# Features of the first layer computed one chunk behind its layernorm, the adjacency diagonal read by one transfer, and the hyperedge table loaded ahead of the feature stores

## The chip, the cores and the metric

One Trainium2 chip, one core. The metric is the device time of one execution in microseconds (us): the median of the runs. Engines are named as in the profile: PE (TensorE, with PEld for its weight loads), DVE (VectorE), ACT (ScalarE), POOL (GpSimd), SP (SyncE, which issues most of the DMAs).

## The reference, cut to what matters

Four graph layers run one after the other on `x` of shape 8 x 2048 x 64, each as `x = x + layer(relu(layernorm(x)))`. Only the start of layer 0 is concerned here.

```python
h = jnp.maximum(_layernorm(x, axis=-1), 0.0)
# layer 0, with H: 2048 nodes x 64 hyperedges
h = x @ W
s = leaky_relu(h @ a_node, 0.2)
logits = where(H.T > 0, s, NEG)          # per batch: 64 hyperedges x 2048 nodes
alpha = softmax(logits, axis=-1)
agg = einsum('ben,bnf->bef', alpha, h)
...
# layer 3 sets adj's diagonal to 1; its degrees and layer 0's deg come from adj
```

## The kernel before, in words

The eight batches are held as four pairs (`NP` = 4, index `q`), each pair with its two 64-wide feature vectors stacked on 128 partitions; the 2048 nodes are cut into four chunks of 512 (`NC`, `CW`, index `ch`) or sixteen tiles of 128 (`NT`, index `t`). A tile framework puts the instructions of each engine in an order of its own, so that work that stands later in the program may be issued between earlier work; each engine then runs its list in order. Blocks under an `If` are not mixed with what stands outside them.

**First stage (`start`, up to 109.6 us).** It has three parts, in this order in the text:

- `layernorm_relu(0, write)`: for each chunk, `norm_parts` centers the four pairs on PE (`center`, tile `bank`), squares and relus them on ACT and DVE (L264, L267, L269), sums the squares on PE (`to_rows`), takes the root on ACT (L272) and the reciprocal on DVE (L273). After its `yield` it spreads that by PE (`from_rows`) and `write` (L553) multiplies on DVE into `hn`. `bank` has six buffers; `xr`, `sq` and `std` have one each.
- `features`: for each chunk, `ph` = `W` applied by feature (four matmuls of 512 columns, copied into `h_t`), then `pn` = the same by node (sixteen of 128 columns, four to a bank, copied into `h_n`). `self.copy` alternates ACT (L172) and DVE (L174).
- `check_adj` and `count_nodes`: the sixteen row blocks of `adj` (1 MB each, four row buffers in `rows`) are loaded by SP (L351). Per block, DVE multiplies the diagonal block by the identity and sums it (`junk`, L352, into `own`), ACT squares the block and sums it (L357), and DVE compares block and square (L358). `squares` has two buffers. Then DVE counts degrees (L362 to L407), PE sums the counts, and a `flag` (L566) is set.

Each `junk`, ACT sum and comparison is followed by a short instruction that reads the accumulator. A register load of `flag` (L2277) then decides the branch. In this execution it is the one with `layer0_pairs`.

**Second stage (`layer0_pairs`).** `aggregate` first stores all of `h_n` to DRAM (`h_rows`, L790, sixteen stores of 256 KB), then forms node scores (L799 to L803) into `score` and `raw`, loads the hyperedge table `HT` into both halves of `cap` (L807, two loads of 512 KB), turns it into caps (L808, L809) and, for each of the four pairs, makes logits by a minimum with `cap` (L818), their maximum (L820), the exponential (L822), transposes and sums. Beside it `ranks`, `hyperedge_keys` (which loads `H`, L520) and `by_rank` make an order of the nodes. `h_rows` is first read by the indirect gathers of POOL (L1797) in the stage after this.

Of the kernel before, what the change touches and what calls it, by code (L numbers as in the profile page):

```python
# [7 lines left out]
F = mybir.dt.float32  # L8
# [5 lines left out]
OP = mybir.AluOpType  # L14
AX = mybir.AxisListType
PSUM = bass.MemoryType.PSUM
# [3 lines left out]
P = 128  # L20
NB = 8
N = 2048
D = 64
NP = NB // 2
NT = N // P
R = P // NP
CW = 512
NC = N // CW
# [99 lines left out]
class Kernel:  # L128
# [36 lines left out]
    def mm(self, out, lhsT, rhs, start=True, stop=True):  # L165
        self.nc.tensor.matmul(out, lhsT, rhs, start=start, stop=stop)  # L166

    def copy(self, out, in_):

        self.flip ^= 1  # L170
        if self.flip:
            self.nc.scalar.copy(out, in_)  # L172
        else:
            self.nc.vector.tensor_copy(out, in_)  # L174
# [164 lines left out]
    def check_adj(self, pool, slots):  # L339


        nc = self.nc
        rows = [slots.tile([P, 2, N], F, name=f"rows{i}", tag=f"q{6 + i}") for i in range(2)]
        squares = slots.tile([P, 2, N], F, name="squares", tag="q8")
        same = pool.tile([P, NT], F, name="same")
        deg = pool.tile([P, NT], F, name="deg")
        own = pool.tile([P, NT], F, name="own")
        junk = pool.tile([P, P], F, name="junk")
        for t in range(NT):
            row, sq = rows[t // 2 % 2][:, t % 2], squares[:, t % 2]  # L350
            nc.sync.dma_start(row, self.a["adj"][t * P : (t + 1) * P])  # L351
            nc.vector.scalar_tensor_tensor(  # L352
                junk, row[:, t * P : (t + 1) * P], 1.0, self.ident, op0=OP.mult, op1=OP.mult,
                accum_out=own[:, t : t + 1],
            )

            nc.scalar.activation(sq, row, AF.Square, accum_out=deg[:, t : t + 1])  # L357
            nc.vector.scalar_tensor_tensor(  # L358
                sq, row, 1.0, sq, op0=OP.mult, op1=OP.is_equal, accum_out=same[:, t : t + 1]
            )  # L360
        bad = pool.tile([P, 1], F, name="bad")
        nc.vector.tensor_reduce(bad, same, axis=AX.X, op=OP.add)  # L362
        nc.vector.tensor_scalar(bad, bad, float(N * NT), None, op0=OP.is_lt)
        nc.vector.tensor_sub(own, deg, own)
        return bad, deg, own
# [178 lines left out]
    def start(self, pool, slots):  # L544

        nc, tc, a = self.nc, self.tc, self.a
        self.deg = pool.tile([P, 2, NT], F, name="deg")
        with tc.tile_pool(reuse_waits="tile", name="k00", bufs=1) as k:
            ww = self.block_diag(k, a["W"], "ww")
            hn = Halves(slots, "hn", ("q0", "q1"), False)  # L550

            def write(q, ch, xr, scale):
                nc.vector.tensor_mul(hn(q)[:, ch * CW : (ch + 1) * CW], xr, scale)  # L553

            self.layernorm_relu(0, write)
            self.features(slots, ww, hn)
            bad, deg, adj_deg = self.check_adj(k, slots)
            flag = pool.tile([1, 1], I32, name="flag")
            with tc.tile_pool(reuse_waits="tile", name="check_ps", bufs=1, space=PSUM) as ps:
                for crowded in self.count_nodes(k, slots, adj_deg):  # L560
                    nc.vector.tensor_max(bad, bad, crowded)
                pt = ps.tile([1, P], F, name="pt")
                nc.tensor.transpose(pt, bad, self.ident)
                one = k.tile([1, 1], F, name="one")
                nc.vector.tensor_reduce(one, pt, axis=AX.X, op=OP.max)
                nc.vector.tensor_scalar(flag, one, 0.0, None, op0=OP.is_gt)  # L566
                nc.vector.tensor_scalar_max(deg, deg, 1.0)
                nc.vector.reciprocal(deg, deg)
                pr = ps.tile([NT, P], F, name="pr")
                nc.tensor.transpose(pr, deg, self.ident)  # L570
                rows = k.tile([NT, P], F, name="rows")
                nc.vector.tensor_copy(rows, pr)
                nc.sync.dma_start(self.rdeg, rows)
        return flag

    def features(self, slots, ww, hn):

        tc = self.tc
        h_t = Halves(slots, "h_t", ("q2", "q3"), False)
        h_n = Halves(slots, "h_n", ("q4", "q5"), True)  # L580
        with (
            tc.tile_pool(reuse_waits="tile", name="h_ps", bufs=3, space=PSUM) as ps,
        ):
            for ch in range(NC):
                for q in range(NP):
                    s = slice(ch * CW, (ch + 1) * CW)
                    ph = ps.tile([P, CW], F, name="ph")
                    self.mm(ph, ww, hn(q)[:, s])
                    self.copy(h_t(q)[:, s], ph)
                for t in range(ch * TC, (ch + 1) * TC):  # L590
                    pn = ps.tile([P, NP, P], F, name="pn")
                    for q in range(NP):
                        self.mm(pn[:, q], hn(q)[:, t * P : (t + 1) * P], ww)
                    self.copy(h_n(t), pn.rearrange("n q f -> n (q f)"))
        self.h = hn, h_t, h_n

    def x_ind(self, slots, k):
# [177 lines left out]
    def aggregate(self, slots, raw, h_t, h_n, fcw, av, both, agg_hi, agg_lo):  # L775
        nc, tc, a = self.nc, self.tc, self.a
        with (
# [7 lines left out]
            for s in range(2):  # L785
                h = slice(s * D, (s + 1) * D)
                nc.vector.tensor_copy(node[h, s : s + 1], self.col("a_node")[h])
                nc.vector.tensor_copy(node[h, 2 + s : 3 + s], self.col("a_gn")[h])
            for t in range(NT):
                nc.sync.dma_start(self.h_rows[t * P : (t + 1) * P, : NB * D], h_n(t))  # L790
            hb = w.tile([P, NT, NB], F, name="hb", bufs=1)

            caps = slots.tile([P, 2, N], F, name="cap", tag="q8")
            cap, score = caps[:, 0], caps[:, 1]
            for ch in range(NC):
                s = slice(ch * CW, (ch + 1) * CW)
                pl = ps.tile([P, CW], F, name="pl")
                self.to_pair_rows(pl, node, lambda q: h_t(q)[:, s])
                nc.scalar.activation(score[:, s], pl, AF.Relu, scale=0.8)  # L799
                nc.vector.scalar_tensor_tensor(  # L800
                    score[:, s], pl, 0.2, score[:, s], op0=OP.mult, op1=OP.add
                )
                nc.scalar.copy(raw[:, s], pl)  # L803

            logits = slots.tile([P, 2, N], F, name="logits", tag="q6")
            for s in range(2):
                nc.sync.dma_start(cap[s * D : (s + 1) * D], a["HT"])  # L807
            nc.vector.tensor_scalar(cap, cap, 0.0, None, op0=OP.is_gt)  # L808
            nc.vector.tensor_scalar(cap, cap, 3e38, NEG, op0=OP.mult, op1=OP.add)  # L809
            aggs = w.tile([P, NP, 2, D], F, name="aggs", bufs=1)  # L810
            nc.gpsimd.memset(aggs, 0.0)
            for q in range(NP):
                lg = logits[:, q % 2]
                for ch in range(NC):
                    s = slice(ch * CW, (ch + 1) * CW)
# [9 lines left out]
                for g in range(NT // 4):  # L825
                    pt = ps1.tile([P, 4, P], F, name="pt")
                    for i in range(4):
                        t = 4 * g + i
# [9 lines left out]
                for s in range(2):  # L838
                    h = slice(s * D, (s + 1) * D)
# [7 lines left out]
                for s in range(2):  # L847
                    h = slice(s * D, (s + 1) * D)
# [20 lines left out]
                for s in range(2):  # L869
                    h = slice(s * D, (s + 1) * D)  # L870
# [7 lines left out]
                for i in range(4):  # L878
                    t = 4 * g + i
# [1057 lines left out]
class Scores:  # L1937
# [27 lines left out]
    def bank(self):  # L1965
        return self.ps.tile([P, CW], F, name="bank", tag="p2")
# [397 lines left out]
```

## Time and profile before

| what | value |
|---|---|
| median of 3 runs | 2153.69 us (2149.0 to 2154.99) |
| profiled execution, its own time | 2148.51 us |
| its span in the trace | 2146.8 us |
| DVE busy, 0 to 81.2 us | 68.9 us |
| ACT busy, 0 to 81.2 us | 50.1 us |
| PE busy, 81.2 to 104.1 us | 22.9 us |
| `flag` set (end of L566) | 109.6 us |
| mean granted TensorE clock | 0.932 |

Times within the execution are microseconds from the first instruction. A row of groups ends in busy time and mean duration of one instruction, then in idle time before them and what ended it. A row of the order in time gives the start, the duration, the engine, the line, the operation and the tiles; in square brackets is the idle time before. A matmul of float32 operands shows in the trace as two PE instructions (the group of `ph` has 32 for sixteen matmuls).

### The profile page before, as it was taken

The numbers are of one execution on the slowest core, as the hardware profiler recorded it, in microseconds if no ns is written. First come the engines' busy times: TensorE is split into PE (matmuls) and PEld (weight loads), VectorE is DVE, ScalarE is ACT, GpSimd is POOL, SyncE is SP. The second block draws the span as 40 slices with busy tenths as digits, with TensorE's granted clock in tenths as the row PEclk, the third lists the DMA queues.
The fourth block names the chain that finished last, engine by engine and source line by source line (L and its number), as shares of the span: only waits on it lengthen the run. The fifth ranks groups of instructions, "written<-read, shape, count | busy, mean of one in ns | idle before, by whom it ended". The sixth has DMA issues, their size and how long they took to land. (4 is left out here: it accounts for less than half of the span.)

```text
span 2146.8 us, 21291 instructions
## 1 busy us (share of the span) xinstructions
PE 1914.5 (89%) x7461; PEld 1153.1 (54%) x7466; DVE 1134.1 (53%) x1932; ACT 714.7 (33%) x1351; POOL 702.4 (33%) x595
## 2 busy tenths in 40 slices
PE   5868999977779999999999998999999999679875
PEld 1425766642237774353443543677777666345432
DVE  7877677737660224424334255698603222249774
ACT  6412555535543440020100201335335333258400
POOL 0000466765300006617357065001000000177770
PEclk8868999988869999999999999999999999879997
DMA  8230333441034360140320401456533443475665
GB/s 320 82 110 4 102 104 118 133 171 43 36 94 134 119 177 14 32 125 0 102 56 5 118 1 60 138 186 235 166 118 125 151 145 131 158 210 162 180 181 180
DMA packets 108797, 253.66 MB, mean 118 GB/s; under 512 B 20912, under 2 KB 21056, under 8 KB 101376
## 3 DMA queue, kind: packets, MB, share of 16 engines
q1 hardware_dynamic: 89264, 181.45, 26.7%
q0 software_dynamic: 17104, 66.47, 10.0%
q10 hardware_dynamic: 2304, 4.20, 0.5%
q8 instruction: 63, 1.03, 0.2%
q14 instruction: 62, 0.51, 0.1%
HBM read 218.30 MB, written 33.78 MB: 117 GB/s over the span
## 5 line engine op out<-in xcount | busy, mean ns | idle before, releaser
L325 ACT CAST adj<-adj_t 128x512 fp32r<-128x512 f32 x384 | 237.3, 619 | 685.9 <-PE pp L166 349.5
L1421 POOL TENSOR_TENSOR acc<-acc,y 128x512 f32<-128x512 f32 x224 | 277.1, 1268 | 444.9 <-DVE y L1416 444.9
L166 PE MATMUL pp<-adj,hi 128*128 128x512 f32 x1280 | 364.4, 404 | 4.4 <-ACT adj L325 4.2
L166 PE MATMUL pk<-q,w 128*128 128x512 f32 (+1 forms) x1024 | 356.5, 609 | 1.8 <-ACT q L1389 1.6
L166 PE MATMUL pp<-adj,lo 128*128 128x512 f32 x1280 | 356.3, 398 | 0.0
L166 PEld LDWEIGHTS pp<-adj,hi 128*128 128x128 f32 x1280 | 241.2, 190 | 77.0 <-issue 16.2
L166 PEld LDWEIGHTS pp<-adj,lo 128*128 128x128 f32 x1280 | 242.7, 190 | 55.6
L166 PEld LDWEIGHTS pk<-q,w 128*128 128x128 f32 (+1 forms) x1024 | 136.2, 188 | 210.2 <-issue 165.9
L1416 DVE SCALAR_TENSOR_TENSOR y<-pk,bias,q 128x512 f32<-128x512 f32 x224 | 157.7, 745 | 142.7 <-PE pk L166 133.2
L166 PE MATMUL acc<-q,ident 128*128 128x512 f32 x416 | 203.4, 615 | 28.4 <-DVE q L2151 16.4
L2061 POOL DMA_INDIRECT ring<-f_rows,near x121 | 140.3, 1160 | 67.5 <-issue 30.2
L166 PEld LDWEIGHTS acc<-q,ident 128*128 128x128 f32 x416 | 76.7, 195 | 104.7 <-issue 47.7
L2165 POOL IOTA q<- 128x2048 int32 x1 | 1.8, 1834 | 316.6 <-PE p L166 316.6
L166 PE MATMUL pp<-adj,x_ind_hi 128*128 128x512 f32 x256 | 94.7, 487 | 2.1 <-DVE q L751 1.9
L166 PE MATMUL bank<-std,from_rows 32*128 32x512 f32 x128 | 45.5, 858 | 54.4 <-DVE std L273 34.5
L1853 POOL TENSOR_TENSOR q<-q,beta 128x512 f32<-128x512 f32 x57 | 67.9, 1192 | 54.6 <-DVE beta L1829 30.8
L1416 DVE SCALAR_TENSOR_TENSOR acc<-pk,bias,q 128x512 f32<-128x512 f32 x32 | 22.6, 746 | 118.1 <-PE pk L166 118.1
L2132 DVE TENSOR_TENSOR q<-ring,e 128x1024 f32<-128x1024 f32 x58 | 70.0, 1218 | 9.3 <-PE acc L166 9.1
L273 DVE RECIPROCAL std<-std 128x512 f32<-128x512 f32 x16 | 53.6, 3351 | 36.7 <-ACT std L272 36.6
L166 PE MATMUL pp<-adj,x_ind_lo 128*128 128x512 f32 x256 | 71.7, 399 | 0.0
L1543 POOL DMA_INDIRECT q<-in_adj_dram,order x15 | 17.2, 1146 | 160.3 <-DVE top L1557 134.0
L166 PEld LDWEIGHTS pp<-adj,x_ind_hi 128*128 128x128 f32 x256 | 48.5, 190 | 38.7 <-issue 23.7
(410 smaller groups left out, 2695.8 us busy)
## 6 DMA issues: line engine op xcount, KB each, us to landing
adj_t<-in_adjT_dram SPq DMA_DIRECT2D x128, 512.0 KB, 3.9
adj_t<-in_adjT_dram SPq DMA_DIRECT2D x128, 256.0 KB, 3.3
rows<-in_adj_dram SPq DMA_DIRECT2D x16, 1024.0 KB, 6.0
q<-x SPq DMA_DIRECT2D x10, 1024.0 KB, 4.8
x<-q SPq DMA_DIRECT2D x9, 1024.0 KB, 4.0
q<-in_embT_dram SPq DMA_DIRECT2D x8, 1024.0 KB, 12.1
x_ch<-in_xT_dram SPq DMA_DIRECT2D x4, 1024.0 KB, 6.0
h_rows<-q SPq DMA_DIRECT2D x16, 256.0 KB, 3.6
```

The source lines that it names most:

```text
L166: self.nc.tensor.matmul(out, lhsT, rhs, start=start, stop=stop)
L273: nc.vector.reciprocal(std, std)
L325: nc.scalar.copy(moving, at[:, i])
L1416: nc.vector.scalar_tensor_tensor(y, pks[b, half], bias[:, b : b + 1], emb[:, b], op0=OP.add, op1=OP.mult,)
L1421: nc.gpsimd.tensor_add(acc, acc, y)
L1543: nc.gpsimd.indirect_dma_start(row, None, self.a["adj"], bass.IndirectOffsetOnAxis(ap=order[:, 1, t : t + 1], axis=0),)
L1853: self.nc.gpsimd.tensor_tensor(x, x, by.unsqueeze(2).to_broadcast([P, NB, D]), op=OP.mult)
L2061: self.nc.gpsimd.indirect_dma_start(to, None, self.kern.f_rows[:], bass.IndirectOffsetOnAxis(ap=index, axis=0))
L2132: nc.vector.tensor_tensor(y.rearrange("n i (b f) -> n i b f", b=NB), block[:, i : i + 2, : NB * D].rearrange("n i (b f) -> n i b f", b=NB) ...
L2165: nc.gpsimd.iota(whole, pattern=[[1, N]], base=0, channel_multiplier=0)
```

## The change

`features` now contains the layernorm's loop. For a chunk it loads `x`, runs `norm_parts` up to its `yield`, computes `ph` of the chunk before, runs the rest of `norm_parts`, and computes `pn` of the chunk before; the last chunk's `ph` and `pn` come after the loop. `bank` has four buffers instead of six, and `ph` and `pn` share four instead of having three each. The copies of chunks 0 to 2 all go to ACT; those of chunk 3 alternate as before. The diagonal of `adj` comes into `own` by one transfer issued by POOL, 128 x 16 single elements, in place of sixteen `junk` instructions. In `aggregate` the two loads of `HT` are issued where the stores of `h_n` were, and the stores come at the beginning of pair 1.

```diff
@@ check_adj
-        junk = pool.tile([P, P], F, name="junk")
+        adj = self.a["adj"]
+        nc.gpsimd.dma_start(
+            own, bass.AP(tensor=adj.tensor, offset=adj.offset, ap=[[N + 1, P], [P * (N + 1), NT]])
+        )
         for t in range(NT):
...
-            nc.vector.scalar_tensor_tensor(
-                junk, row[:, t * P : (t + 1) * P], 1.0, self.ident, op0=OP.mult, op1=OP.mult,
-                accum_out=own[:, t : t + 1],
-            )
@@ start
-            self.layernorm_relu(0, write)
-            self.features(slots, ww, hn)
+            self.features(slots, ww, hn, write)
@@ features
-            tc.tile_pool(reuse_waits="tile", name="h_ps", bufs=3, space=PSUM) as ps,
+            tc.tile_pool(reuse_waits="tile", name="ln", bufs=2) as w,
+            tc.tile_pool(reuse_waits="tile", name="ln_ps", bufs=1, space=PSUM) as ps,
...
+            def copy(ch, to, src):
+
+                if ch < NC - 1:
+                    self.nc.scalar.copy(to, src)
+                else:
+                    self.copy(to, src)
+
+            for ch in range(NC):
+                x = self.load_x(w, 0, ch)
+                xr = w.tile([P, NP, CW], F, name="xr", bufs=1)
+                sq = w.tile([P, NP, CW], F, name="sq", bufs=1)
+                std = w.tile([P, CW], F, name="std", bufs=1)
+                norm = self.norm_parts(ch, x, xr, sq, std, bank, write)
+                next(norm)
+                if ch > 0:
+                    by_feature(ch - 1)
+                next(norm, None)
+                if ch > 0:
+                    by_node(ch - 1)
+            by_feature(NC - 1)
+            by_node(NC - 1)
@@ aggregate
-            for t in range(NT):
-                nc.sync.dma_start(self.h_rows[t * P : (t + 1) * P, : NB * D], h_n(t))
...
+            for s in range(2):
+                nc.sync.dma_start(cap[s * D : (s + 1) * D], a["HT"])
             for ch in range(NC):
...
-            for s in range(2):
-                nc.sync.dma_start(cap[s * D : (s + 1) * D], a["HT"])
...
             for q in range(NP):
+                if q == 1:
+                    for t in range(NT):
+                        nc.sync.dma_start(self.h_rows[t * P : (t + 1) * P, : NB * D], h_n(t))
```

More of the change, by code (lines that the diff above doesn't have):

```diff
@@ L574, in start, with features @@
         return flag
-    def features(self, slots, ww, hn):
+    def features(self, slots, ww, hn, write):
         tc = self.tc
@@ L581, in features, with bank, by_feature, by_node @@
         with (
-            tc.tile_pool(reuse_waits="tile", name="h_ps", bufs=3, space=PSUM) as ps,
-        ):
-            for ch in range(NC):
+            tc.tile_pool(reuse_waits="tile", name="ln", bufs=2) as w,
+            tc.tile_pool(reuse_waits="tile", name="ln_ps", bufs=1, space=PSUM) as ps,
+        ):
+            def bank():
+                return ps.tile([P, CW], F, name="bank", bufs=4)
+            def by_feature(ch):
+                s = slice(ch * CW, (ch + 1) * CW)
                 for q in range(NP):
-                    s = slice(ch * CW, (ch + 1) * CW)
-                    ph = ps.tile([P, CW], F, name="ph")
+                    ph = ps.tile([P, CW], F, name="ph", tag="h", bufs=4)
                     self.mm(ph, ww, hn(q)[:, s])
-                    self.copy(h_t(q)[:, s], ph)
+                    copy(ch, h_t(q)[:, s], ph)
+            def by_node(ch):
                 for t in range(ch * TC, (ch + 1) * TC):
-                    pn = ps.tile([P, NP, P], F, name="pn")
+                    pn = ps.tile([P, NP, P], F, name="pn", tag="h", bufs=4)
                     for q in range(NP):
                         self.mm(pn[:, q], hn(q)[:, t * P : (t + 1) * P], ww)
-                    self.copy(h_n(t), pn.rearrange("n q f -> n (q f)"))
+                    copy(ch, h_n(t), pn.rearrange("n q f -> n (q f)"))
+            def copy(ch, to, src):
[17 more added lines that the diff above has]
+            by_node(NC - 1)
         self.h = hn, h_t, h_n
```

## The prediction

> **What bounds the kernel now.** I read first the busy time of the engines by stretch (columns: length, then busy microseconds and instruction count of PE, PEld, DVE, ACT, POOL, then the granted TensorE clock, the DMA share, GB/s), with stretches cut at events taken from the order in time: a chunk's spread of the reciprocals (21.4, 37.9, 54.4, 68.8), the end of the check of `adj` (81.2), the end of the features (104.1), the flag (109.7), and the wait for `HT`.
>
> ```profile
> core 0: us, PE busy (x) PEld busy (x) DVE busy (x) ACT busy (x) POOL busy (x), PEclk, DMA share, GB/s
> ...
> 21.40:37.90 16.50, 10.01 (x27) 2.79 (x27) 16.50 (x24) 12.84 (x17) 0.00 (x0) 0.81 0.98 374
> 37.90:54.40 16.50, 9.92 (x28) 2.87 (x28) 16.50 (x26) 11.50 (x15) 0.00 (x0) 0.81 0.75 267
> 54.40:68.80 14.40, 10.17 (x24) 2.88 (x24) 14.34 (x22) 9.50 (x13) 0.00 (x0) 0.84 0.83 279
> 68.80:81.20 12.40, 9.74 (x31) 4.26 (x32) 12.40 (x20) 5.58 (x7) 0.00 (x0) 0.72 0.01 2
> 81.20:104.10 22.90, 22.90 (x139) 17.17 (x139) 14.35 (x58) 7.67 (x14) 0.00 (x0) 1.00 0.00 1
> 104.10:109.70 5.60, 1.12 (x7) 0.33 (x5) 4.67 (x45) 0.00 (x0) 0.00 (x0) 0.74 0.01 1
> ...
> 124.00:130.40 6.40, 0.58 (x1) 0.00 (x0) 0.06 (x1) 0.00 (x0) 0.00 (x0) 0.50 0.99 210
> ```
>
> Up to 81.2 us DVE never rests: it bounds. PE works 10 of 16 us there, at a clock of 0.81. From 81.2 to 104.1 PE alone bounds, with the features and nothing else. From 124.0 to 130.4 all five engines stand still while DMA runs at 0.99. The whole program's chain of waits covers only its last instructions, so the chain here is read from the order in time:
>
> ```profile
> 68.84 1.74 PE L166 MATMUL bank<-std,from_rows 32*128 32x512 f32 x8 [4.17 <-DVE std L273]
> ...
> 78.90 2.29 DVE L358 SCALAR_TENSOR_TENSOR squares<-rows,squares 128x2048 f32<-128x2048 f32 x1
> ...
> 83.16 3.60 PE L166 MATMUL ph<-q,ww 128*128 128x512 f32 x8
> ...
> 100.60 3.73 PE L166 MATMUL pn<-ww,q 128*128 128x128 f32 x32
> ...
> 104.18 0.26 PE L166 MATMUL pn<-least,ones 128*128 128x224 bf16 x1
> ...
> 109.47 0.14 DVE L566 TENSOR_SCALAR flag<-one 1x1 int32<-1x1 f32 x1
> ```
>
> A chunk of features is 3.6 + 3.7 us of PE, 7.0 from one `ph` block (83.05) to the next (90.05). DVE's own part of the counting is done at 90.4 (end of L568, from 90.19), but the count's matmul stands behind the features in PE's list and waits until 104.2. In the second stage, from the waits, the order in time and the DMA issues (last column: issue to landing):
>
> ```profile
> DVE cap L808 <- DMA cap<-in_HT_dram: 6.7, 1, 6.7
> ...
> 111.65 9.14 SPq L790 DMA_DIRECT2D h_rows<-q  x16
> 120.83 1.23 SPq L807 DMA_DIRECT2D cap<-in_HT_dram  x2
> ...
> cap<-in_HT_dram SPq DMA_DIRECT2D x2, 512.0 KB, 7.5
> ...
> h_rows<-hb SPq DMA_DIRECT2D x1, 64.0 KB, 3.0
> ```
>
> `HT` is issued after sixteen stores and lands behind their 4 MB; the first maximum (L820) can only follow it.
>
> **What the Trainium skill says.** "ScalarE: Activation LUTs", section "What ACT_TABLE_LOAD costs": 186 ns + 0.833 ns per element for an ACTIVATE with immediates, so 612 ns at 512; the trace's copies take 585, so it agrees. A switch of tables would be dear, but copies at 75.3 us already follow the root of L272 with no load before them, so the moved copies bring none. "TensorE: Matmul & The Clock Gate", section "The HAM clock gate", gives half rate after idling; here PE instructions of 512 columns step by 0.86 us (9.72 to 10.57) in the layernorm and 0.43 in dense features. "DMA: Bandwidth & Descriptors", section "Rules for kernel authors": a strided last dimension is one descriptor per element, so the diagonal is 2048 of them; "Issuing engines are not separate DMA queues": POOL's transfer runs on the same 16 engines as SP's loads. The trace before has no such transfer.
>
> **The change, part by part.**
>
> *Features behind the layernorm.* Three chunks, 3 x 7.0 = 21.0 us of PE work, move from the bare stretch into the layernorm's. There PE is busy 39 us of the 62.6 from 7.9 to 70.5 (47.2 up to 81.2, less 8.2 of features), so 23.6 are idle. That is only just enough, unless the fuller PE keeps its clock: part of its 0.86-us steps would become 0.43. Two limits follow.
>
> DVE's limit: the last comparison's accumulator is read at 81.2. Sixteen `junk` with their reads cost 0.2 each from start to next start (23.63 to 23.84, 40.12 to 40.33), 3.2 in all. One feature copy before 81.12 goes, 0.6. So the check ends at 77.3. From 81.12 to 90.4 DVE takes 9.3, of which six copies are 6 x 0.6 = 3.6; 5.7 stay, and chunk 3's four DVE copies (2.4) join: 85.4. From the count's matmul to the flag is 5.5 (104.1 to 109.6), less one copy inside, 0.6: 4.9. Flag at **90.3**.
>
> PE's limit: the spreads at 21.4 and 68.8 are three chunks of 15.8 us apart. A chunk gains 0.6 from three missing `junk`. It loses where `bank` has four buffers: two pairs of the next chunk were centered before the writes were through (39.91), now they wait for them, and `pn` (3.7 us) of the chunk behind stands first; the fourth square then comes about 1.5 us later. ACT's list is in order, and eight copies a chunk (0.5 us each in a row) stand among the squares; a stretch's 9.5 to 12.8 us of ACT become 13.5 to 16.8, full in the first. I take 0.9 more for that, within 0 and 3. Net +1.8 a chunk: last spread at 68.8 + 5.4 = 74.2. Then spread 2.1, `pn` of chunk 2 3.7, `ph` and `pn` of chunk 3 7.3: 87.3, and 4.9 to the flag: **92.2**. The later limit holds; gain 109.6 - 92.2 = **17.4**. Its ends: 21 if all three chunks' PE time vanishes, 11 if each chunk loses 4 (6.4 more than the 5.4 above).
>
> *Table loads, PSUM, SP.* The `x` loads keep their place in SP's list between row loads; `x` of chunk 3 was issued at 28.5 and used after 54, so nothing is late. The copies taken from DVE in the bare stretch were hidden by PE; moving them is worth 0 beyond the sum above.
>
> *Diagonal.* Removed: the 3.2 us counted above. Added: one POOL issue; POOL has nothing to do until 110.4, so its time is hidden. `own` is read at 82.4 (L364). On the DMA engines, the nearest row is the store of `hb`: 2048 runs of 32 bytes, 3.0 us to landing, where an 8 KB store needs 1.4, so 1.6 us of transfer, 12.5 ns for each of 128 runs per engine. The elements meet the first `x` load, which everything waits for until 7.9 us, and DVE's limit starts there. Bounds: 0 (landed before or after it) and 3; I take **1.0** lost. A gain from it is excluded, since nothing that it replaces used DMA.
>
> *`HT` first.* It moves two issues (1.23 us of SP) ahead of sixteen (9.14). The stores now stand behind `HT` and `H`; who waits for them is the gather L1797 at 213.7, over 80 us after the latest place they can take, and in SP's list only the two loads of `w_ind`, first used at 213.3, are behind. `HT` issued 1.3 us after the branch lands 3 to 4 us later, before the scores (L800) are through at 122.5. So the wait of 6.7 goes. What is late next: DVE itself, 13.0 of 13.3 us from 130.4 to 143.7, and 53.7 of 66.3 after it, with PE 62.3. Filling DVE's small gaps with L808 and L809 (2.5 us) may add to it; a cold PE behind the first logits may take some back. Bounds 3 and 9; I take **6.7**.
>
> **Sum**: 17.4 - 1.0 + 6.7 = 23.1 us. Against the profiled execution: 2148.5 - 23.1 = 2125.4. That execution lies 5.2 below the median, at the bottom of the runs; the same saving from the median gives 2130.6.
>
> **The rivals.**
>
> *PE and ACT become the bound, in their order.* Copies wait at the head of ACT's list for cold matmuls, squares come late, and DVE idles. For it: PE's 39 + 21 us in 62.6, and ACT already squares 1.91 us a block. Against: the framework mixes the lists, and half the clock is to be won back. At 5 us lost per chunk instead of 1.8 the flag comes 9.6 later: gain 13.5, **2140**.
>
> *The instructions move little.* The first-stage order was already free to be mixed (the check is), so the new text could give nearly the old list, with only `HT` and the `junk` helping: DVE wins nothing while PE still does 28 us after 75.2. Gain 6.7, **2147**. Against: the features could not start early because the layernorm's six banks and their own six exceed eight, and the last `write` freed them.
>
> *The diagonal's elements jam the DMA engines* (the slower side). DMA's share from 0 to 68.8 adds up to 58.6 us of full work. If an element cost 0.4 us instead of 0.0125, 128 x 0.4 = 51 us join: the last row block lands at 2.5 + 58.6 + 51.2 = 112.3, then square and comparison 4.2, DVE's 5.7 and 4.9: flag at 127.1, 17.5 later than now. With 6.7 from `HT`: **2164**. It decides from 0.32 us an element (no net gain), and over 0.3% from 0.37. Against: the `hb` row, 30 times cheaper; for: that row reads SBUF, and these read single words 8 KB apart.
>
> **How the numbers follow.** About 0.3%, 6.5 us, can be told from no change here. Forecast 0.70; PE and ACT bound 0.15; little moved 0.08, half of it inside 0.3%; jam 0.07. Faster 0.87, same 0.07, slower 0.06 (a mild jam counts as same). The forecast's ends: gains of 11 - 3 + 3 = 11 and 21 + 9 = 30, with runs 3 us apart either way: 2121 to 2146. It takes in the first rival and most of what is left out is the jam; the range is 2120 to 2147.
>
> **What would show it.** In the changed profile: `ph` and `pn` of chunks 0 to 2 between the spreads, with ACT's copies of them at 585 ns and only chunk 3's four on DVE; spreads about 17.6 us apart; TensorE clock above 0.9 from 20 to 75 us; one 7-us block of features after the last spread; flag at 91 to 95; no wait of L808 on `HT` and the first exponential some 20 us after the branch; `own` landed long before L364. Wrong would be DVE idling on squares or on rows in the first 80 us, PE still full for over 12 us before the flag, or a first `x` that lands after 11 us.

## The result, and the profile after

| | before | after |
|---|---|---|
| median of runs shown | 2152.06 us (4 runs) | 2132.57 us (4 runs, 2128.78 to 2135.07) |
| ratio | 1 | 0.9912, 95% interval 0.9894 to 0.9931 |
| profiled execution, span | 2146.8 us | 2129.6 us |
| flag set | 109.6 us | 95.1 us |
| first exponential of the second stage (start) | 143.7 us | 120.6 us |
| first `x_ind` copy, where the next stage begins | 216.5 us | 197.7 us |

The change is faster by 19.5 us of the medians; the forecast was 23.1 us and 2130.6 us. Two places gained, as forecast: 14.5 us up to the flag, 4.3 more up to the first `x_ind` copy. The spans differ by 17.2, 1.6 less than these 18.8.

First the busy time of the engines by stretch, cut again at the chunks' spreads (23.0, 41.5, 57.9, 72.5), at the end of the check (84.5) and at the flag (95.1); columns as in the prediction:

```profile
23.00:41.50 18.50, 17.01 (x58) 7.62 (x58) 16.24 (x16) 14.17 (x21) 0.00 (x0) 0.70 0.86 326
41.50:57.90 16.40, 15.54 (x71) 7.99 (x70) 16.12 (x16) 15.45 (x25) 0.00 (x0) 1.00 0.81 292
57.90:72.50 14.60, 13.17 (x61) 6.47 (x60) 14.43 (x14) 13.94 (x22) 0.00 (x0) 1.00 0.80 263
72.50:84.50 12.00, 9.68 (x57) 6.50 (x57) 11.37 (x16) 8.15 (x13) 0.00 (x0) 1.00 0.01 1
84.50:88.50 4.00, 0.05 (x1) 0.00 (x0) 4.00 (x28) 0.00 (x0) 0.00 (x0) 0.58 0.00 0
88.50:95.10 6.60, 1.50 (x4) 0.27 (x3) 5.79 (x65) 0.00 (x0) 0.00 (x0) 0.50 0.01 1
```

The bare stretch of 22.9 us of PE is gone. PE now works 13 to 17 us of each chunk, and from 41.5 to 84.5 at full clock (1.00, where it was 0.72 to 0.84 up to the end of the check). DVE rests 0.3 us or less in each of the next two chunks and 0.6 in the stretch after them, so it is the candidate for the bound of the stage; ACT is nearly full too, 15.45 of 16.4, and experiments below tell the two apart. The longest wait of DVE lies between 23.0 and 41.5 (2.3 us), where the clock was 0.70.

The order in time of DVE and PE at the end of the stage:

```profile
80.88 2.05 PE L166 MATMUL pn<-ww,q 128*128 128x128 f32 x16 [0.75 <-ACT q L172]
81.05 0.68 DVE L174 COPY q<-ph 128x512 f32<-128x512 f32 x1
81.65 0.68 DVE L174 COPY q<-pn 128x512 f32<-128x512 f32 x1
82.25 2.28 DVE L357 SCALAR_TENSOR_TENSOR squares<-rows,squares 128x2048 f32<-128x2048 f32 x1
84.45 0.68 DVE L174 COPY q<-pn 128x512 f32<-128x512 f32 x1
...
88.45 0.35 PE L166 MATMUL pn<-least,ones 128*128 128x224 bf16 x1 [5.52 <-DVE least L370]
...
94.96 0.14 DVE L564 TENSOR_SCALAR flag<-one 1x1 int32<-1x1 f32 x1
```

PE is through with the features at 82.9. The wait has turned round: before, the count's matmul stood behind the features in PE's list; now PE waits 5.5 us for DVE's classes (L370). Three feature copies stand ahead of the last comparison (L357) in DVE's list.

In the second stage, SP's issues, DVE's cap table and the exponentials:

```profile
97.06 1.18 SPq L820 DMA_DIRECT2D cap<-in_HT_dram  x2
98.47 0.40 SPq L519 DMA_DIRECT2D twice<-in_H_dram  x1
98.98 14.36 SPq L839 DMA_DIRECT2D h_rows<-q  x16
...
105.16 1.22 DVE L832 TENSOR_SCALAR cap<-cap 128x2048 f32<-128x2048 f32 x1
...
120.58 2.00 ACT L849 ACTIVATE logits<-logits,mx 128x2048 f32<-128x2048 f32 x1
...
139.59 2.00 ACT L849 ACTIVATE logits<-logits,mx 128x2048 f32<-128x2048 f32 x1 [1.82 <-DVE mx L847]
```

L832 no longer waits for `HT`. The stores do not come at pair 1, whatever their place in the text: SP issues them right behind `H`, at 99 us, and they take 14.4 us of SP instead of 9.1. The first exponential comes 25.5 us after the flag instead of 34.1, but the second follows after 19.0 instead of 17.1.

### The profile page after: what moved, and what is told of

It reads as the page before. It is cut to its first block, busy times and chain, and to the rows that moved or that the text cites. A ratio compares the mean times of both kernels' runs of the same rounds, so it can differ in the third digit from the quotient of the medians.

```text
span 2129.6 us, 21268 instructions
## 1 busy us (share of the span) xinstructions
PE 1907.2 (90%) x7462; PEld 1149.7 (54%) x7466; DVE 1123.1 (53%) x1888; ACT 719.3 (34%) x1363; POOL 706.3 (33%) x596
## 5 line engine op out<-in xcount | busy, mean ns | idle before, releaser
L1570 POOL DMA_INDIRECT q<-in_adj_dram,order x15 | 17.2, 1147 | 161.7 <-DVE top L1584 135.0
L1535 DVE SCALAR_TENSOR_TENSOR q<-p,cols,q 128x512 f32<-128x512 f32 x16 | 12.0, 751 | 108.4 <-PE p L166 107.5
```

Of the source, the lines that this page charges most:

```text
L1535: nc.vector.scalar_tensor_tensor(x[:, q], p2, self.col("b2"), x[:, q], op0=OP.add, op1=OP.add)
L1570: nc.gpsimd.indirect_dma_start(row, None, self.a["adj"], bass.IndirectOffsetOnAxis(ap=order[:, 1, t : t + 1], axis=0),)
```

## The experiments

The kernels ran on several chips, and the later stages differ between them by more than the effects sought (the first kernel below has the shorter second stage and yet a span of 2162.6 us). So places in the first 220 us are compared, and ratios are given beside them. Kernels with the same first stage show how far the flag wanders: 109.6 (before), 110.6, 109.6 and 111.8 in the three that leave that stage alone; 95.1 and 94.4 with the changed one.

**`HT` alone.** Only `aggregate` is changed: its three hunks of the change.

```diff
-            for t in range(NT):
-                nc.sync.dma_start(self.h_rows[t * P : (t + 1) * P, : NB * D], h_n(t))
...
+            for s in range(2):
+                nc.sync.dma_start(cap[s * D : (s + 1) * D], a["HT"])
```

> The kernel before with only the loads of HT moved ahead of the stores of h_n and the stores put at pair 1; the first stage is unchanged, so the flag stays at 109.6 us. Theory (a gain at the first exponential, part of it given back because VectorE's order work is only put off): first exponential about 8 us earlier than before's 143.7, the store of the last node scores (209.7 before) about 5 us earlier, whole execution 4 to 5 us shorter. Rival (the wait of 6.7 us goes for good): the last store 6.7 us or more earlier and the whole execution 6.7 us or more shorter.

Measured: flag 110.6; first exponential at 134.8, 24.3 us after the flag (34.1 before); the last scores' store 94.5 us after the flag (100.0 before); first `x_ind` copy 102.6 after it (106.9 before). So 9.8 us are gained at the first exponential and 4.2 kept in this trace. Ratio 0.9956, 0.994 to 0.9971; by its interval the whole gains 6.3 to 13 us, more than this pair of traces accounts for.

**Features alone.** `features` and `start` as changed, `check_adj` and `aggregate` as before.

> The kernel before with only the features behind the layernorm and copied by ScalarE; the diagonal is still multiplied out on VectorE, and HT still comes after the stores. Theory (after the change VectorE bounds the first stage again, so the 16 diagonal multiplications count in full): flag 2 to 3 us later than after the whole change, at 97 to 98 us instead of 95.1, so 12 us earlier than before. Rival (TensorE and ScalarE bound the first stage): the multiplications fit into VectorE's waits and the flag is at 95 us or earlier. Second stage as before: the wait on HT of 6 to 7 us is there.

Measured: flag at 100.5, later than either theory had it; ratio 0.9929, 0.9906 to 0.9953. The first line of the cap table still waits 5.7 us for `HT`. The last comparison starts at 88.2 instead of 82.3. Of the 9.1 us gained against before's 109.6 the features are the whole. Keeping the multiplications cost 5.4 us against the whole change, but not all of that is their own time. Between the second and the last comparison, where DVE bounds, fourteen of them stand, 2.9 us at 0.2 each; there DVE also waited 6.6 us instead of 3.4, most of it for the root of the second chunk, whose spread came 21.7 us after the first instead of 18.6:

```profile
39.69 3.35 DVE L273 RECIPROCAL std<-std 128x512 f32<-128x512 f32 x1 [4.27 <-ACT std L272]
```

The start was 0.6 earlier. So 2.9 us are the multiplications' own and 3.2 are longer waits, whether caused by them or by another order of the lists; that isn't separated. The rival falls: the multiplications did not fit into DVE's waits.

**Diagonal alone.** `check_adj` as changed, the rest as before.

> The kernel before with only the diagonal's transfer in place of the 16 multiplications. Theory: TensorE's features behind the layernorm set the flag in this form, so VectorE's 3.2 us free most of nothing: the layernorm's chunks come about 0.6 us earlier each, the first x about 1 us later, flag within 2 us of 109.6. Rival (VectorE's time is what counts even here): flag 3 us earlier. Second rival (the single words jam the DMA engines): flag later by over 2 us.

Measured: first matmul at 8.7 instead of 7.9; last comparison starting at 76.2 instead of 78.9; flag at 108.8; ratio 0.998, 0.9966 to 0.9994. DVE is 2.7 us earlier through its check and it is worth 0.8, inside the scatter of the flag, because the count's matmul starts at 103.4, behind PE's features. The same edit whose absence costs 5.4 us behind the features is worth next to nothing alone.

**Last chunk's copies on ACT too.**

```diff
-                if ch < NC - 1:
-                    self.nc.scalar.copy(to, src)
-                else:
-                    self.copy(to, src)
+                self.nc.scalar.copy(to, src)
```

> The changed kernel with the last chunk's eight copies on ScalarE too, instead of alternating. Theory (VectorE bounds the end of the first stage, and its four copies stand ahead of the last comparisons and counts): flag 2 us earlier, at about 93 us, and the whole 2 us shorter. Rival (ScalarE's squares come later by its four more copies, 2.4 us, and the last comparison waits for them): flag at 95 us or later.

Measured: flag at 91.8, 3.3 us earlier; about 1.0 of that is the second chunk (40.5 to the spread instead of 41.5), so 2.3 are the copies. Ratio 0.9903, 0.9875 to 0.9931. DVE's list in order of time:

```profile
75.03 2.28 DVE L357 SCALAR_TENSOR_TENSOR squares<-rows,squares 128x2048 f32<-128x2048 f32 x1
...
77.24 2.29 DVE L357 SCALAR_TENSOR_TENSOR squares<-rows,squares 128x2048 f32<-128x2048 f32 x1
...
79.45 2.29 DVE L357 SCALAR_TENSOR_TENSOR squares<-rows,squares 128x2048 f32<-128x2048 f32 x1
```

The comparisons stand back to back, and ACT's squares are in time with four more copies on it.

**All copies alternating.**

```diff
-                if ch < NC - 1:
-                    self.nc.scalar.copy(to, src)
-                else:
-                    self.copy(to, src)
+                self.copy(to, src)
```

> The changed kernel with the copies of all four chunks alternating between ScalarE and VectorE as before, instead of chunks 0 to 2 on ScalarE. Theory (VectorE bounds the first stage): twelve more copies of 0.6 us on it, flag 6 to 7 us later than the changed kernel's 95.1, at 101 to 102. Rival (ScalarE bounds it, relieved here of twelve copies): flag at 95 us or earlier.

Measured: flag at 104.0, 8.9 us later; ratio 0.9936, 0.9913 to 0.9959. Twelve copies of 0.6 us are 7.2 of it; the other 1.7 are waits of DVE (5.0 us between its second and last comparison instead of 3.4). Relieving ACT bought nothing and loading DVE cost it in full: DVE bounds the changed stage.

**PSUM ring.**

```diff
-                return ps.tile([P, CW], F, name="bank", bufs=4)
+                return ps.tile([P, CW], F, name="bank", bufs=6)
...
-                    ph = ps.tile([P, CW], F, name="ph", tag="h", bufs=4)
+                    ph = ps.tile([P, CW], F, name="ph", tag="h", bufs=2)
```

> The changed kernel with six buffers for bank and two for ph and pn, instead of four and four. Theory (the ring of four costs next to nothing now, since TensorE ends before VectorE): spreads of the four chunks no closer than 18.6, 16.4 and 14.5 us by more than 1 us in all, flag within 1.5 us of 95.1, later rather than earlier because ph and pn have fewer buffers. Rival (as the forecast had it, the ring makes each chunk's last square 1.5 us late): spreads 1 to 1.5 us closer each, flag 2 us or more earlier.

Measured: spreads 17.2, 20.7 and 15.0 us apart against 18.6, 16.4 and 14.5, flag at 94.0, ratio 0.9894 (0.9868 to 0.992). Counted from the first, the last spread comes later by 3.3 us and yet the flag is 1.1 earlier: the spreads are not what sets it. Here PE's features end at 88.3 and the count's matmul stands right behind them (88.1), but DVE has work meanwhile and rests only 0.6 us from its last comparison to the flag. The edit changes two rings at once. Six buffers with two for the copies are no better within the scatter of the flag, so a cost of four shows neither way.

**Diagonal's transfer later.** A one-column copy makes it wait for the fifth row block's sum.

```diff
-        nc.gpsimd.dma_start(
-            own, bass.AP(...)
-        )
...
+            if t == 4:
+                nc.gpsimd.tensor_copy(own[:, :1], deg[:, t : t + 1])
+                nc.gpsimd.dma_start(own, bass.AP(...))
```

> The changed kernel with the diagonal's transfer issued only after the fifth row block has been squared (a one-column copy on GpSimd makes it wait), so that it does not meet the first loads. Theory (the single words cost the first x load about 1 us): first matmul at 7.9 us instead of 9.0 and flag about 1 us earlier, at 94. Rival (they cost nothing there, or cost the row loads the same later): first matmul at 9, or flag unchanged at 95 or later.

Measured: first matmul at 7.9, first spread at 22.3 instead of 23.0, flag at 93.3; ratio 0.991, 0.9878 to 0.9941. Of the 1.8 us at the flag 0.6 lie ahead of the first spread, and 1.2 in the second chunk (17.4 instead of 18.6), which wanders by as much between kernels that are alike there. Over all kernels the first matmul starts at 8.6 to 9.0 us where the transfer stands first (six) and at 7.8 to 7.9 otherwise (eight), so its cost to the first load, 0.9 on average, is clear. At the flag it is 1.8 here and, with the last chunk's copies on ACT, 0 and 0.9 (91.8 without the delay, 91.8 and 90.9 with it in the last two experiments). The changed kernel's DMA queues up to the flag (packets, MB, share of 16 engines) and its issue (KB, us to landing):

```profile
q0 software_dynamic: 48, 0.01, 1.0%
...
own<-in_adj_dram POOLq DMA_DIRECT2D x1, 8.0 KB, 5.0
```

1.0% of 95 us is 0.95 us of all engines. In the three kernels that issue it later the same transfer shows 0.3 to 0.8 us and 4.3 to 7.6 us to landing, so the figure is not the transfer's alone. The 2048 single words went in 48 packets; the profile does not show descriptors.

**Half the order's comparisons on POOL**, on the kernel before, and the same with `HT` first.

```diff
-                nc.vector.tensor_scalar(hot, line, here[:, t : t + 1], None, op0=OP.is_equal)
+                engine = nc.gpsimd if t % 2 else nc.vector
+                engine.tensor_scalar(hot, line, here[:, t : t + 1], None, op0=OP.is_equal)
```

> The kernel before with 32 of the 64 comparisons that make the order's one-hot rows (L532, 0.42 us each) moved from VectorE to GpSimd, which is idle then; 13 us leave VectorE between the flag and the store of the last node scores. It is the base for the next run. Theory (VectorE's order work is the filler that the second stage must finish): that store comes some 3 to 8 us earlier than the 100.2 us after the flag of before. Rival (each pair's own chain sets the stage): under 2 us earlier.

> The run before this one with HT ahead of the stores as well. Theory (the gain of 9 us at the first exponential is partly given back only because VectorE has put off its order work): with half of that work gone, 7 us or more of the 9 stay, counted from the flag to the store of the last node scores against the run before this. Rival (the gain is given back by the pairs' chain itself, or by the stores in DMA): 5 us or less stay, as without GpSimd's help.

These don't decide. The instructions that write `hot`, from the first of the two kernels (ns: least, median, most):

```profile
L533 DVE TENSOR_SCALAR hot<-linef,rank_here x32: 471/488/901, 121.3 to 208.9; 128x512 bf16<-128x512 f32 x32
L533 POOL TENSOR_SCALAR hot<-linef,rank_here x32: 1551/1561/1898, 121.4 to 211.2; 128x512 bf16<-128x512 f32 x32
```

POOL takes 1.56 us for what DVE does in 0.49. The last scores' store came 111.3 us after the flag instead of 100.0 (ratio 1.0031, 1.0019 to 1.0044), and with `HT` first 108.2 (1.0017, 1.0003 to 1.0031). It isn't simply POOL's pace: in the first of the two POOL itself waited 28.3 us for PE to read `hot` buffers, and PE 6.8 for POOL. How the three hold each other up was not separated. 3.1 us of `HT`'s gain stay there, in a stage that is no longer the same one.

**One put-off comparison on POOL.** Of the work that slid behind the first exponential, `by_rank`'s 128 x 2048 comparison is the largest piece (2.3 us).

```diff
-        nc.vector.tensor_tensor(
-            here, line.unsqueeze(1).to_broadcast(full), lowf[:, 1].unsqueeze(2).to_broadcast(full),
-            op=OP.is_equal,
-        )
+        for t in range(NT):
+            nc.gpsimd.tensor_scalar(here[:, t], line, lowf[:, 1, t : t + 1], None, op0=OP.is_equal)
```

> The changed kernel with the order's 128x2048 comparison in by_rank (2.3 us on VectorE, part of the work put off past the first exponential) done in 16 pieces on GpSimd, where nothing waits for it in the pairs' loop. Theory (work put off on VectorE is what gives back 4 of the 9 us): from the flag to the first x_ind copy 1.5 to 2.5 us less than the 102.6 after the change. Rival (the pairs' own chain gives it back): within 0.7 us of 102.6.

Measured: flag at 94.4, first `x_ind` copy 101.9 after it instead of 102.6, so the rival's answer: taking 2.3 us from DVE there bought 0.7 at most, and the second stages of seven kernels with `HT` first scatter from 100.1 to 102.6. The whole is slower (ratio 0.995, 0.9932 to 0.9967) because `by_rank` serves layer 3 as well, where its comparison is waited for: from the last store of `x` to the first gather of that layer 45.6 us instead of 39.6.

**Three edits together**: copies on ACT, transfer later, and the comparison on POOL.

> The changed kernel with three edits together: the last chunk's copies on ScalarE as well, the diagonal's transfer behind the fifth row block, and by_rank's comparison on GpSimd. Theory (all three take load off VectorE or the first load, and add up): flag at 91 us and the first x_ind copy at 192 instead of 197.7, whole 5 us shorter than the changed kernel. Rival (the comparison on GpSimd saves nothing): first x_ind copy at 193.5 or later.

Measured: flag at 91.8, first `x_ind` copy at 194.7, ratio 0.994, 0.9917 to 0.9962. The flag is that of the copies on ACT alone (91.8): the later transfer added nothing to it here. The comparison on POOL saves nothing.

**Two edits together**, without POOL's comparison.

> The changed kernel with the last chunk's copies on ScalarE as well and the diagonal's transfer behind the fifth row block; by_rank as in the changed kernel, since its GpSimd form is used a second time in layer 3 and cost 6 us there. Theory (both edits take load off VectorE or the first load, and VectorE sets the flag): flag at 91 to 92.5 us, first x_ind copy 100 to 102.7 us after it, whole some 3 us shorter than the changed kernel, ratio to the kernel before near 0.990. Rival (ScalarE's squares come late by its extra copies): flag at 95 us or later.

Measured: flag at 90.9, first `x_ind` copy at 191.8 (100.9 after it), median 2130.59 us, ratio 0.9911, 0.9895 to 0.9928. In the trace it is 5.9 us ahead of the changed kernel at the first `x_ind` copy; over whole runs its ratio cannot be told from the changed kernel's 0.9912.

## Why the prediction was right, and which of its terms were off

Of the signs it named, the wait of L808 went, `own` landed at 6.6 us (read at 85.1), only chunk 3's four copies stood on DVE, and the flag lies at the end of its range. Others failed: the clock from 23.0 to 41.5 was 0.70 and not above 0.9, and the first exponential came 25.5 us after the flag and not some 20.

**Features.** The move hides 21 us of PE beside DVE, as said, and PE ran at full clock from 41.5 to 84.5. But the prediction let PE's limit, 92.2, decide over DVE's, 90.3, and both were off the other way. That the sum came near the measured flag is partly luck: the limit taken for the later one was passed early, and the other came 4.8 us late.

PE's end came to 82.9 where 87.3 was worked out: the spreads were 18.6, 16.4 and 14.5 us apart (17.6 expected), and at full clock the last chunk needed 10.4 us after its spread instead of 13.1. The terms of 0.9 for ACT and of 1.5 for `bank`'s four buffers are not seen as such: only the second chunk grew, and the kernel with six did not do better. (The forecast's lower end has a slip: three chunks at 4 are 6.6 more than 5.4, not 6.4; the gain of 11 stands.)

DVE's check ended at 84.5 instead of 77.3, 7.2 later: 1.1 us of later start; 0.7 more up to the second comparison; 3.3 us of waiting from there on, 2.2 of them where the root waited for PE; and 1.8 for three copies that the framework put ahead of the last comparison, which the prediction had counted behind it (so they shift the term, not the flag). This leaves 0.3. "Up to 81.2 us DVE never rests" holds only from 21.4 on: before, it worked 7.4 of the 13.5 us up to there, and the first of the sixteen multiplications stood in a wait, so it freed nothing. From the check's end to the flag 13.0 us were summed with all four copies (5.7 + 2.4 + 4.9) and 10.6 measured with one of them: 10.0 against 10.6 without any, so these steps held within 0.6.

The wait in the second chunk reads so in the order of time (the bracket at a line's end names what was waited for):

```profile
35.72 1.06 PE L166 MATMUL bank<-sq,to_rows 128*32 128x512 f32 x8
...
36.91 0.69 ACT L272 ACTIVATE std<-bank,eps 128x512 f32<-128x512 f32 x1 [0.49 <-PE bank L166]
37.63 3.35 DVE L273 RECIPROCAL std<-std 128x512 f32<-128x512 f32 x1 [2.25 <-ACT std L272]
```

The sums of squares stood in PE's list behind centering and the first of `ph`, which stepped by 0.86 us up to 33.9; in the next chunk centering steps by 0.43. That is the place where the rival of PE and ACT in their order was right, for one chunk of three.

**Diagonal.** 1.0 us lost was forecast, bounds 0 to 3; the first `x` came 1.1 later and DMA spent 0.95 us on it. The jam did not happen: 0.95 us for 128 words on each engine is 7.4 ns a word, below the 12.5 of the forecast's nearest row; the later transfers needed less. That the multiplications were worth 3.2 us held only behind the features, where 2.9 are their own time; alone the edit gave 0.8 at the flag.

**`HT`.** The wait went, and 6.7 us were forecast with bounds of 3 and 9. The pair of profiles gives 4.3. Over all kernels whose second stage is one of the two, the first `x_ind` copy comes 100.1 to 102.6 us after the flag with `HT` first (seven, mean 101.2) and 105.3 to 109.5 without (three, mean 107.2): 6.0. The forecast's term is right within that scatter. `HT` took 6.3 us to landing and not 3 to 4, which cost nothing, as no instruction waited for it. What it didn't see is that 9.6 us are gained at the first exponential (24.2 after the flag against 33.9 on average) and 3.6 given back by the first `x_ind` copy. So its 6.7, the length of one wait, came near the net of a larger gain and a loss.

The given-back part is only partly explained. Busy time before and after the first exponential says that work was put off: before,

```profile
109.61:143.67 34.06, 17.98 (x51) 4.81 (x53) 25.54 (x76) 5.79 (x9) 2.23 (x8) 0.60 0.56 173
143.67:209.65 65.98, 61.99 (x329) 39.49 (x332) 53.57 (x128) 17.74 (x31) 0.00 (x0) 0.84 0.00 1
209.65:216.49 6.84, 5.18 (x22) 3.98 (x21) 4.13 (x15) 1.65 (x5) 2.22 (x3) 0.72 0.39 86
```

and after,

```profile
95.10:120.58 25.48, 17.04 (x47) 4.56 (x48) 20.04 (x62) 5.80 (x10) 2.23 (x8) 0.57 0.77 231
120.58:189.39 68.81, 63.10 (x329) 39.82 (x332) 56.61 (x137) 17.64 (x31) 0.00 (x0) 0.81 0.00 1
189.39:197.66 8.27, 6.04 (x27) 3.77 (x26) 7.18 (x28) 1.65 (x6) 3.48 (x4) 0.80 0.36 67
```

DVE does 83.2 and 83.8 us in the three stretches together, but 5.5 us of it moved from ahead of the first exponential to behind it, and 3.1 of those lie after the last store of scores, where five one-hot comparisons were still to be made. The end of the stage, before,

```profile
212.54 0.69 DVE L541 TENSOR_TENSOR key<-bank,mt 128x512 bf16<-128x512 f32 x1
213.29 1.77 SPq L313 DMA_DIRECT2D adj_t<-in_adjT_dram  x4
```

and after,

```profile
194.73 0.69 DVE L540 TENSOR_TENSOR key<-bank,mt 128x512 bf16<-128x512 f32 x1 [0.17 <-PE bank L166]
195.48 1.76 SPq L313 DMA_DIRECT2D adj_t<-in_adjT_dram  x4
```

`key` ends the chain of the order: one-hot comparisons, their matmuls, a running sum. In all fourteen traces SP's first load of the next stage follows its end by 0.06 to 0.15 us, and in twelve PE's first matmul for `x_ind` by 0.05 to 0.10, which reads as their release. `key` ends 3.6 us after the last store of scores in the three kernels without `HT` first and 5.9 to 6.1 after it in the seven with it. That is where about half of the 3.6 us goes: from the last store to the copy it takes 8.2 to 8.3 us in the seven and 5.8 to 6.8 in the three, 1.8 more on average. In the kernel with `by_rank`'s comparison on POOL two one-hot comparisons stand behind the store and `key` ends 4.4 after it, but the copy gains only 0.8 of that: the pairs' own last matmuls are then still in PE's list ahead of those for `x_ind`. So work put off on DVE is the cause of this half, read from the order in time; no experiment moved these comparisons alone. The other half lies between the first exponential and the last store (68.7 us on average against 66.9, where the three without `HT` first range from 66.0 to 68.6) and is not told from the scatter; its cause, and the part that PE's clock has in it (0.84 to 0.81), stays open.

**The sum.** Forecast 23.1; the traces have 14.5 + 4.3 = 18.8 at the first `x_ind` copy. 1.9 of the shortfall is the first stage (16.4 forecast), 2.4 the second stage in this pair, 0.7 if its mean of 6.0 is taken. The remaining 1.6 us between 18.8 and the spans' 17.2 arise after that copy, where no instruction was changed and runs of one kernel differ by 6 us.

## What to carry to other kernels

Before crediting work that is moved beside other work, add up each engine's own list to the same end point; here the engine that bounded the covered stretch came to bound the stage, and its small jobs, worth next to nothing until then, counted in full. A load that is soon waited for belongs ahead of bulk stores whose reader comes late; credit it with the gain at the end of the stage, since part of what the first waiter gains can be given back. A framework that orders instructions itself may ignore the place that the text gives a DMA with free inputs: read the issue times.

## What the runs showed of the hardware

2048 single 4-byte words 8196 bytes apart, loaded by one POOL transfer, took 1.34 us of POOL, 0.95 us of the DMA engines and 5.0 us to landing beside the first full loads; in the three kernels that issued it later it took 0.3 to 0.8 us of the engines and 4.3 to 7.6 to landing. The same comparison of 128 x 512 float32 to bf16 took 1.56 us on POOL and 0.49 on DVE. With the features beside it, from 41.5 us on, the layernorm ran at a PE clock of 1.00, where it had 0.81 to 0.84 without them: the third chunk's centering then steps by 0.43 to 0.53 us from one instruction to the next (43.8 to 46.9), where its first two steps took 1.0 and 0.85 before (39.9 to 41.8). More work made the old work faster there, but not in the chunk before (23.0 to 41.5), where PE was busy 17.0 of 18.5 us at a clock of 0.70.
